# Two layers of graph attention over 64 graphs: the first two graphs in a new order, with zero products, logits from x, and TensorE transposes

## The chip, the cores and the metric

The kernel runs on one core of a Trainium2 chip, in one launch. The metric is the device time of one execution in microseconds, as the median of several runs. A separate execution was recorded by the hardware profiler; times inside the kernel are from that one.

## The reference, cut to what matters

There are 64 independent graphs of N = 256 nodes with F = 512 features, H = 8 heads of U = 64. All of it is float32.

```python
def layer0(X, A, W, b, a_self, a_neigh):                 # graph attention
    feats = einsum('bnf,hfu->bhnu', X, W)
    e_self, e_neigh = einsum('bhnu,hu->bhn', feats, a_self), einsum('bhnu,hu->bhn', feats, a_neigh)
    dense = leaky_relu(e_self[..., :, None] + e_neigh[..., None, :], 0.2)
    att = softmax(dense + -1e10 * (1.0 - A[:, None]), axis=-1)
    out = einsum('bhij,bhju->bhiu', att, feats) + b
    return relu(rows_of_heads_side_by_side(out))         # (64, 256, 512)

def layer1(x, mask, A, D, W_qkv, W_out, b_out):          # A and D are both adj here
    q, k, v = heads(x @ W_qkv)
    dots = where(mask_pair, einsum('bhid,bhjd->bhij', q, k) / 8, -big)
    attn = softmax(dots) * 0.33 + 0.33 * where(mask_pair, A, 0) + 0.33 * exp(-where(mask_pair, D, big))
    return rows_of_heads_side_by_side(einsum('bhij,bhjd->bhid', attn, v)) @ W_out + b_out

x = layernorm(x + layer0(x, adj, ...))
x = layernorm(x + layer1(x, nodemask, adj, adj, ...))
```

## The kernel before

The work on one graph is cut into named steps in six groups: `turned` (x transposed), `proj0` (features, logits and softmax factors of layer 0), `attend0` (attention of layer 0 and its normalisation), `proj1` (q, k and v of layer 1), `softmax1` and `attend1`. `do(stage, b, step)` issues one step for graph b. After each, `in_order()` ties every new instruction to the one before it on its engine, so the order in which the calls stand in `start()` and in the two loop functions is the order in which each engine executes. There is no planner. Engines wait for one another by semaphores; DMAs go to SP's queue, which takes them in order too.

The steady loop handles several graphs at once: `attention0_beside_projections1(b)` does the attention of layer 0 for graph b, q, k and v of graph b-1 and the features of graph b+1; `attention1_beside_projections0(b)` does the softmax of graph b-1 and the attention of layer 1 for graph b-2. `start()` fills this pipeline for graphs 0 and 1, then the loop runs for b = 1 to 63 and `end()` empties it.

Products of the steady loop use Strassen's scheme with seven products per two-by-two blocks (`seven`, named p1 to p7), for which VectorE prepares sums: `left_factors` of the data (steps `xC`, `hC`) and `right_factors` or `combine_weights1` of the weights. The first two graphs' features use plain products (`features(t, g)`: tile t of 128 nodes, half g of the heads), since the weight sums aren't there yet. All matmuls of L87 go through `halved`, which splits the 128 weight columns into two halves. In the records of the trace one float32 matmul is two (a transpose one).

In layer 0 the softmax needs two logits per node and head. For graph 1 and on they come as two more columns (`U:` up to `UX`) of the feature product, because `attention_vectors(g, step)` puts W times the attention vectors into the weights: step 0 transposes four weight blocks on TensorE (`pw`, L412) and copies them on ScalarE (`wT`), step 1 multiplies them with `a2` (`pwa`, L424, 4 columns), step 2 copies the result into the weights `wf` (L429). For graph 0 `logits(t, g)` computes them on VectorE from the features and `a_bc`, the attention vectors broadcast to 128 partitions (L631, L636). `copied` adds the bias and moves features out of the accumulator (L641). `maxima` transposes the logits (`pr`, L90), takes the maximum over nodes (L554) and forms the exponent; with part 1 it spreads the maxima by a product with `sel` (`pn`, L546). `columns` makes the column factors (L582, L589, L590). `factors` spreads the row factors to all partitions by products of 8 rows with `sel` (`pg`, L576); from graph 2 on, `rows` and `broadcast` do this through DRAM (`gs`, then `gb`). `scaled` scales the features on ScalarE (L649), `weights` forms the attention weights on VectorE (`pT`, L692, two per head), `product` multiplies them (`av`, L715).

Graph 0's outcome of layer 0 is divided on VectorE (L736, L738), that of the others by ScalarE: `rec0` takes reciprocals on VectorE (L728) and `norm0` scales eight heads per half on ScalarE (L746, 16 instructions). `end`, `squares` and `norm` make the layer norm. The outcome is then needed transposed for q, k and v (`hT`). For graph 0 TensorE transposes it (`from_rows`, `ph`, L90); for the others it is written to DRAM (`blocks`: `hs`, then four block loads into `hb`) and VectorE transposes it (step `hT`, L129). Values of layer 1 are `pv` (L87), copied out or added by ScalarE and VectorE (`v`, L331 and L334); the sums of the softmax are `pd` (L925). Four accumulator banks (`tag="mm"`, `bufs=4`) are shared by nearly all of these, so a product waits until a bank's last reader is done.

## Time and profile before

| | us |
|---|---|
| runs (3) | 2845.17, 2847.23, 2848.95; median 2847.23 |
| profiled execution | 2844.27, its span 2842.5 |
| TensorE busy, in the span | 2808.4 (99%) |
| VectorE, ScalarE, GpSimd busy | 2562.7, 1806.8, 252.6 |
| first feature product of graph 1 starts at | 38.69 |
| first attention product (`av`) of graph 1 | 66.63 |
| first feature product of graph 2 (`pf_p`) | 84.00 |
| first attention product of graph 2 | 111.64 |
| first value product (`pv_p`) of graph 1, of graph 2 | 122.08, 165.21 |

Times are counted from the start of the span. An execution's own time is a little longer than the span, which runs from the first to the last recorded instruction. PE is TensorE's matmuls, PEld its weight loads, DVE VectorE, ACT ScalarE, POOL GpSimd, SP the queue that issues DMAs. PEclk, or the column behind the busy times in a table of stretches, is the granted share of TensorE's full clock; behind it stand the DMA engines' busy share and GB/s. In a timeline a line gives start and length in us, engine, source line, operation, tiles, shape and count, and in brackets the idle time before it and who ended it.

### The profile page before, as it was taken

What the parts mean: (1) busy time and instruction counts of PE and PEld (TensorE: products, weight loads), DVE (VectorE), ACT (ScalarE), POOL (GpSimd) and SP (SyncE); (2) the same over time, 40 slices, a digit from 0 to 9 for tenths busy, and PEclk for the clock granted to TensorE, in tenths of its full rate; (3) what the DMA queues carried; (4) which work ended last, traced back from release to release, by engine and by line L of the source; (5) the groups of instructions that cost most, each with busy time, mean ns of one, the idle gap of its engine ahead of it and who ended that gap; (6) DMA issues with size and microseconds to landing.
All of it is one profiled execution on the core that took longest, in us unless ns stands there. A gap on an engine that the chain in (4) does not pass through costs nothing.

```text
span 2842.5 us, 93477 instructions
## 1 busy us (share of the span) xinstructions
PE 2808.4 (99%) x39110; PEld 2237.5 (79%) x39110; DVE 2562.7 (90%) x5147; ACT 1806.8 (64%) x5031; POOL 252.6 (9%) x526
## 2 busy tenths in 40 slices
PE   9899999999999999999999999999999999999998
PEld 7688787887888888877877878878778778778775
DVE  6799999999999999999999999999999999999984
ACT  3566666666666666666666666666666666666663
POOL 0001000100101000010000001001000100100011
PEclk9999999999999999999999999999999999999999
DMA  6345454454454454454554544554554545544532
GB/s 140 91 129 123 133 141 121 132 144 121 126 137 126 130 140 118 136 134 124 140 122 132 144 121 128 141 127 126 137 124 131 141 119 137 134 126 138 122 113 71
DMA packets 778972, 363.87 MB, mean 128 GB/s; under 512 B 694605, under 2 KB 696637, under 8 KB 762553
## 3 DMA queue, kind: packets, MB, share of 16 engines
q1 hardware_dynamic: 776440, 357.37, 48.3%
q8 instruction: 310, 5.08, 0.8%
q14 instruction: 110, 0.89, 0.1%
q10 hardware_dynamic: 2112, 0.52, 0.1%
HBM read 289.42 MB, written 68.13 MB: 126 GB/s over the span
## 4 chain that ended last, share of the span: by engine, by line
PE 96%; DVE 2%; DMA 1%; ACT 1%; issue 0%; SPq 0%; POOL 0%; DVEq 0%; POOLq 0%
PE pq_p L87 27%; PE po_p L87 14%; PE pf_p L87 13%; PE pv_p L87 13%; PE av L715 8%; PE pz L886 8%; PE av L1015 7%; PE pd L925 2%; PE pr L510 1%; PE po L87 0%; DMA x<-in_x_dram 0%; PE pg L576 0%; DMA hb<-hs 0%; PE pf L87 0%; SPq L122 0%
## 5 line engine op out<-in xcount | busy, mean ns | idle before, releaser
L87 PE MATMUL pq_p<-hC,wqk_sb 128*64 128x128 f32 x8192 | 472.3, 273 | 1.9 <-ACT qk L331 1.7
L87 PEld LDWEIGHTS pq_p<-hC,wqk_sb 128*64 128x64 f32 x8192 | 450.6, 137 | 4.5 <-ACT qk L331 2.8
L692 DVE SCALAR_TENSOR_TENSOR pT<-gb,ccol,at 128x256 f32<-128x256 f32 x992 | 403.0, 477 | 17.5 <-ACT ccol L589 17.5
L87 PE MATMUL pq_p<-hT,wqk_sb 128*64 128x128 f32 x6144 | 358.0, 273 | 0.0
L87 PEld LDWEIGHTS pq_p<-hT,wqk_sb 128*64 128x64 f32 x6144 | 342.4, 137 | 9.6 <-issue 0.4
L905 ACT ACTIVATE p<-pz,hide 128x512 f32<-128x512 f32 x638 | 333.6, 629 | 8.0 <-PE pz L886 1.0
L996 DVE TENSOR_TENSOR p<-p,rb 128x1024 f32<-128x1024 f32 x252 | 299.0, 1207 | 3.3 <-DMA rb<-rs 3.3
L1005 DVE TENSOR_TENSOR p<-p,ct 128x1024 f32<-128x1024 f32 x252 | 299.0, 1206 | 0.2
L746 ACT ACTIVATE x<-av,rec 128x64 f32<-128x64 f32 x1008 | 220.9, 335 | 68.3 <-DVE rec L728 68.3
L87 PE MATMUL pv_p<-wv_sb,hC 128*64 128x256 f32 x2048 | 246.7, 382 | 9.5 <-ACT v L331 9.5
L715 PE MATMUL av<-v,pT 128*64 128x65 f32 x8192 | 254.0, 223 | 1.3 <-issue 1.0
L87 PE MATMUL pf_p<-wf_sb,xC 128*64 128x264 f32 x1984 | 254.5, 386 | 0.0
L715 PEld LDWEIGHTS av<-v,pT 128*64 128x64 f32 x8192 | 250.6, 139 | 2.2 <-issue 2.0
L649 ACT ACTIVATE v<-v 128x64 f32<-128x64 f32 x1024 | 251.2, 336 | 0.0
L331 ACT COPY qk<-pq_p 128x512 f32<-128x512 f32 x256 | 149.0, 582 | 150.5 <-PE pq_p L87 147.3
L1015 PE MATMUL av<-p,v 128*64 128x256 f32 x2016 | 240.6, 379 | 2.1 <-DVE p L1005 2.1
L886 PE MATMUL pz<-qk 64*128 64x256 f32 x2048 | 238.8, 383 | 0.0
L331 ACT COPY v<-pv_p 128x256 f32<-128x256 f32 x256 | 95.7, 374 | 224.8 <-PE pv_p L87 224.8
L87 PE MATMUL po_p<-wo_sb,oC 128*64 128x256 f32 x1984 | 235.2, 379 | 0.0
L385 POOL TENSOR_SCALAR rstd_l<-rstd_l 128x2 f32<-128x2 f32 (+1 forms) x130 | 95.6, 736 | 1539.5 <-ACT junk L374 1539.5
L886 PEld LDWEIGHTS pz<-qk 64*128 64x128 f32 x2048 | 192.3, 186 | 45.1 <-issue 24.6
L87 PEld LDWEIGHTS pv_p<-wv_sb,hC 128*64 128x64 f32 x2048 | 154.9, 138 | 79.2 <-ACT v L331 10.4
(165 smaller groups left out, 4471.1 us busy)
## 6 DMA issues: line engine op xcount, KB each, us to landing
rb<-rs SPq DMA_DIRECT2D x63, 1024.0 KB
gb<-gs SPq DMA_DIRECT2D x62, 1028.0 KB
hs<-x SPq DMA_DIRECT2D x64, 512.0 KB
xb<-in_x_dram SPq DMA_DIRECT2D x252, 128.0 KB
x<-in_x_dram SPq DMA_DIRECT2D x63, 512.0 KB
hb<-hs SPq DMA_DIRECT2D x252, 128.0 KB
y<-hs SPq DMA_DIRECT2D x63, 512.0 KB
out_dram<-y SPq DMA_DIRECT2D x63, 512.0 KB
```

Of the source, the lines that this page charges most:

```text
L87: matmul(dst[cols], lhsT[:, cols], rhs, **flags)
L331: nc.scalar.copy(out[COPIES[p]], dst)
L385: nc.gpsimd.tensor_scalar(rstd, rstd, 1.0 / F, EPS, op0=ALU.mult, op1=ALU.add)
L649: nc.scalar.activation(V0[b][:, t, h, :U], V0[b][:, t, h, :U], AF.Copy, scale=V0[b][:, t, h, U : U + 1],)
L692: nc.vector.scalar_tensor_tensor(pT[h][:, j, :], GB[b][h], CCOL[b][:, j, h : h + 1], AT[b][:, j, :], op0=ALU.max, op1=ALU.mult,)
L715: matmul(av[r * half : (r + 1) * half, k, :], pT[h][:, j, i : i + half], V0[b][:, j, h, :UA], start=(j == 0), stop=(j == T - 1),)
L746: nc.scalar.activation(X1[b][:, t, h * U : (h + 1) * U], av[:, k, :U], AF.Copy, scale=REC0[g][:, t, k : k + 1],)
L886: matmul(pz[r][:, j, :], QK[b][rows, g, 1, j * P : (j + 1) * P], QK[b][rows, g, 0, :], start=True, stop=True,)
L905: nc.scalar.activation(to, of, AF.Exp, bias=hide[:, j, b : b + 1], scale=U**-0.5,)
L996: nc.vector.tensor_mul(p, p, REC[b][:, k : k + 2, g // 2, :] .unsqueeze(2) .to_broadcast([P, 2, T, N]),)
L1005: nc.vector.tensor_add(p, p, CT[b].unsqueeze(1).to_broadcast([P, 2, T, N]))
L1015: matmul(av[0][r * U : (r + 1) * U, g % 2, :], V1[b][:, j, 2 * g + r, :], PROBS[b][g][:, r, j, :], start=(j == 0), stop=(j == T - 1),)
```

## The change

Only the beginning is changed: what is done for graphs 0 and 1, and the loop, which now starts at b = 2. The instructions of the steady loop and of `end()` stay as they are.

- Zero products: `keep_busy(dst, n)` issues n matmuls of a 128x128 block of zeros with itself into an accumulator that is overwritten right after. There are 19: six before the mask's transposes, four before those of x, and for graph 0 three each before the transposes of the logits, the product that spreads the maxima and the first product that spreads the row factors. The zeros lie in `rowmask`, which is filled much later.
- Logits of graph 0 from x: all four weight blocks are transposed at once (`turned_weights`), multiplied with the attention vectors (`attention_vectors`, 16 products), copied into `wa`, and `logits()` multiplies x with that (8 products of 16 columns). `vectors_placed` copies `wa` into the weights later. The two broadcast loads of `a_bc` and VectorE's products and reductions are gone; `a2` is filled by GpSimd.
- Loads: x of graph 0 in one DMA ahead of the mask's instead of two behind it; the adjacency of graph 1 is loaded after the step `aT` at its new place.
- Order of `start()`: logits and factors come before most of graph 0's features; graph 1's row factors are spread in two halves; the weight sums for q and k come later.
- `second_beside_first()` takes the place of the loop's pass for b = 1: reciprocals and scaling of graph 1 first, VectorE's transposes of graph 2 and the sums for `wf` after or between, `right_factors` in parts.
- Graph 1's outcome is transposed by TensorE (`from_rows`), written to DRAM but not loaded as blocks.

The lines removed from `start` and `attention_vectors` are those of the listing above.

```diff
+    load_rows(0)
     mask_sb = io.tile([NB, N], U8, tag="mask", name="mask_sb", bufs=4)
     nc.sync.dma_start(mask_sb, nodemask)
-    X[0] = io.tile([P, T, F], FT, tag="hb", name="x_0", bufs=1)
-    for t in range(T):
-        nc.sync.dma_start(X[0][:, t, :], x[0, t * P : (t + 1) * P, :])
...
-    a_bc = io.tile([P, 2, H, U], FT, tag="x1", name="a_bc", bufs=1)
...
+    rowmask = consts.tile([P, NB // B, N // B, B], FT, name="rowmask")
+    idle = rowmask[:, 0, : P // B].rearrange("p i b -> p (i b)")
+    nc.vector.memset(idle, 0.0)
...
+    for r in range(2):
+        rows = slice(r * U, (r + 1) * U)
+        nc.gpsimd.tensor_copy(a2[rows, :, r, :].rearrange("p g s -> p s g"), acol[rows])
...
+    def keep_busy(dst, n):
+
+        for _ in range(n):
+            matmul(dst, idle, idle, start=True, stop=True)
+
+    keep_busy(ps_tile([P, P], "pi"), 6)
...
-    def right_factors(w, w12):
+    def right_factors(w, w12, steps=range(4)):
...
+        for i in steps:
+            if i == 0:
+                nc.vector.tensor_add(m3, w22, w12)
...
...
+    def turned_weights(g):
+
+        pw = ps_tile([P, C, P], f"pw_{g}")
+        for c in range(C):
+            for r in range(2):
+                matmul(
+                    pw[r * U : (r + 1) * U, c, :],
+                    wf[c // C2][g // 2][:, c % C2, 2 * (g % 2) + r, :U],
+                    ident,
+                    start=True,
+                    stop=True,
+                )
+        tag = "both" if g < HG - 1 else "pT"
+        wT = WA[g] = work.tile([P, C, P], FT, tag=tag, name=f"wT_{g}", bufs=4)
+        nc.scalar.copy(wT, pw)
+        in_order()
+
+    def attention_vectors():
...
+        pwa = ps_tile([P, C, HG, 4], "pwa")
+        for g in range(HG):
             for c in range(C):
+                matmul(pwa[:, c, g, :], WA[g][:, c, :], a2[:, g], start=True, stop=True)
+        wa = WA["columns"] = work.tile([P, C, H, 2], FT, tag="hC", name="wa", bufs=1)
+        nc.vector.tensor_copy(
+            wa.rearrange("p c h s -> p (c h s)"), pwa.rearrange("p c g k -> p (c g k)")
+        )
+        in_order()
+
+    def vectors_placed():
+
+        for k in range(2):
+            for g in range(2):
                 nc.vector.tensor_copy(
+                    wf[k][g][:, :, :, U:],
+                    WA["columns"][:, k * C2 : (k + 1) * C2, g * HG : (g + 1) * HG],
                 )
         in_order()
...
                 pt = ps_tile([P, C, P], f"pt_{b}_{t}")
+                if t == 0:
+                    keep_busy(pt[:, 0, :], 4)
...
         def maxima(part=None):
             if part == 1:
-                ROW["max"] = ps_tile([P, H], f"pn_{b}")
+                pn = ps_tile([P, P], f"pn_{b}")
+                if b == 0:
+                    keep_busy(pn, 3)
+                ROW["max"] = pn[:, :H]
                 matmul(ROW["max"], sel[:, H, :], ROW["diag"], start=True, stop=True)
                 return
-            ps = ps_tile([H, 2, N], f"pr_{b}")
+            ps = ps_tile([P, 2, N], f"pr_{b}")
+            if b == 0:
+                keep_busy(ps[:, 0, :P], 3)
+            ps = ps[:H]
...
-        def factors():
+        def factors(part=None):
...
+            if part != 1:
+                nc.vector.tensor_scalar(
+                    grow[:, :N], grow[:, :N], 1.0, TINY, op0=ALU.min, op1=ALU.max
+                )
+                GB[b] = []
+
+            h = HG if part == 1 else 0
+            while h < (HG if part == 0 else H):
                 n = 2 if b == 0 and h < HG else HG
                 if n == 2:
                     pg = ps_tile([P, n, N], f"pg_{b}_{h}")
                 else:
                     pg = psum.tile([P, n, N], FT, tag="sc", name=f"pg_{b}_{h}", bufs=2)
+                if b == 0 and h == 0:
+                    keep_busy(pg[:, 0, :P], 3)
                 for k in range(n):
                     matmul(pg[:, k, :], sel[:, h + k, :], grow[:, :N], start=True, stop=True)
                     GB[b].append(pg[:, k, :])
...
-        def logits(t, g):
...
+        def logits():
+
+            pl = ps_tile([P, T, H, 2], f"pl_{b}")
+            for t in range(T):
+                for c in range(C):
+                    matmul(
+                        pl[:, t],
+                        xT[:, c, t * P : (t + 1) * P],
+                        WA["columns"][:, c],
+                        start=(c == 0),
+                        stop=(c == C - 1),
+                    )
+            nc.vector.tensor_copy(V0[b][:, :, :, U:], pl)
...
         def rows_to_blocks():
             nc.sync.dma_start(HS[b].rearrange("(t p) f -> p t f", p=P), X1[b])
-            if b > 0:
+            if b > 1:
                 load_blocks(hb, HS[b])
...
         tiles = [slice(t, t + 1) for t in range(T)]
         do("proj0", 0, "xT_rows")
+        for g in range(HG):
+            turned_weights(g)
+        do("proj0", 0, "features", 0, 0)
+        attention_vectors()
+        do("proj0", 0, "logits")
+        do("proj0", 0, "copied", 0, 0)
+        do("proj0", 0, "maxima")
+        do("proj0", 0, "aT")
+        load_adj(1)
+        do("proj0", 0, "features", 1, 0)
+        do("proj0", 0, "maxima", 1)
+        do("proj0", 0, "columns")
+        do("proj0", 0, "far")
+        do("proj0", 0, "factors")
+        do("proj0", 0, "features", 0, 1)
+        do("proj0", 0, "features", 1, 1)
+        do("proj0", 0, "copied", 1, 0)
+        for h in range(HG):
+            do("proj0", 0, "scaled", h)
+            do("attend0", 0, "weights", h)
+        do("proj0", 0, "copied", 0, 1)
+        do("proj0", 0, "copied", 1, 1)
+        for h in range(HG, H):
+            do("proj0", 0, "scaled", h)
+        for t in range(T):
+            do("attend0", 0, "product", 0, t)
+        for h in range(HG, H):
+            do("attend0", 0, "weights", h)
+        vectors_placed()
+        do("turned", 1, "xT")
+        load(2)
+        for t in range(T):
+            do("attend0", 0, "product", 1, t)
         for g in range(2):
             for t in range(T):
...
+                do("proj0", 1, "features", t, g)
         for t in range(T):
             for g in range(2):
                 do("attend0", 0, "norm0", g, t)
             do("attend0", 0, "end", tiles[t])
             do("attend0", 0, "squares", tiles[t])
...
         do("proj0", 1, "copied", 0, 0)
-        combine_weights1(0)
-        do("proj0", 1, "copied", 0, 1)
-        combine_weights1(4)
         do("proj0", 1, "copied", 1, 0)
         do("proj0", 0, "shared", 0)
+        do("proj0", 1, "copied", 0, 1)
         do("proj0", 1, "aT")
         do("proj0", 1, "copied", 1, 1)
+        do("proj0", 1, "maxima")
         do("proj1", 0, "from_rows", 0)
         do("proj1", 0, "from_rows", 1)
         do("proj1", 0, "blocks")
         load_rows(1)
-        do("proj0", 1, "maxima")
-        do("proj1", 0, "qk", "p1")
         do("proj0", 1, "maxima", 1)
         do("proj0", 1, "columns")
-        do("proj1", 0, "qk", "p2")
-        do("proj1", 0, "hC")
-        do("proj0", 1, "factors")
+        do("proj1", 0, "qk", "p1")
+        do("proj0", 1, "factors", 0)
         do("proj0", 0, "shared", 1)
         do("proj0", 1, "far")
         load_adj(2)
+        combine_weights1(0)
+        combine_weights1(4)
+        do("proj1", 0, "qk", "p2")
+        do("proj1", 0, "hC")
         do("proj1", 0, "qk_add", 11)
+        do("proj1", 0, "qk", "p6")
         combine_weights1(1)
-        do("proj1", 0, "qk", "p6")
         for h in range(HG):
             do("proj0", 1, "scaled", h)
             do("attend0", 1, "weights", h)
-        combine_weights1(2)
         do("proj1", 0, "qk", "p5")
         do("proj1", 0, "qk", "p7")
+        do("proj0", 1, "factors", 1)
         for h in range(HG, H):
             do("proj0", 1, "scaled", h)
+        combine_weights1(2)
         do("proj1", 0, "qk_add", 22)
         for h in range(HG, H):
             do("attend0", 1, "weights", h)
         do("proj1", 0, "qk", "p3")
         do("proj1", 0, "qk_add", 12)
         combine_weights1(3)
...
+    def second_beside_first():
+
+
+        b = 1
+        for g in range(2):
+            for t in range(T):
+                do("attend0", b, "product", g, t)
+        do("attend0", b, "rec0", 0)
+        do("attend0", b, "rec0", 1)
+        load_rowmask()
+        nc.sync.dma_start(bo_bc, b_out.partition_broadcast(P))
+        WO["12"] = load_wo()
         do("turned", 2, "xT")
         do("turned", 2, "xC")
-        right_factors(wf_sb, wf12)
-        in_order()
+        for t in range(T):
+            do("attend0", b, "norm0", 0, t)
+        do("proj1", 0, "values", "p1")
+        for t in range(T):
+            do("attend0", b, "norm0", 1, t)
+        do("proj1", 0, "values", "p2")
+        do("proj1", 0, "v_add", 11)
+        do("attend0", b, "end")
+        right_factors(wf_sb, wf12, (0, 1, 2))
+        do("proj1", 0, "values", "p6")
+        do("proj1", 0, "values", "p5")
+        do("proj1", 0, "values", "p7")
+        do("proj1", 0, "v_add", 22)
+        right_factors(wf_sb, wf12, (3,))
+        load(3)
+        do("proj0", 2, "product", "p1")
+        do("proj1", 0, "values", "p4")
+        do("attend0", b, "squares", slice(0, 1), False)
+        do("proj0", 2, "product", "p6")
+        do("attend0", b, "squares", slice(1, 2), slice(0, 2))
+        do("proj1", 0, "values", "p3")
+        do("proj0", b, "shared")
+        do("proj0", 2, "aT")
+        do("proj1", 0, "v_add", 12)
+        do("proj0", 2, "product", "p5")
+        do("proj0", 2, "product", "p7")
+        do("attend0", b, "norm")
+        do("proj1", b, "blocks")
+        do("proj0", 2, "add", 22)
+        do("proj0", 2, "product", "p2")
+        do("proj0", 2, "product", "p4")
+        do("proj0", 2, "far")
+        do("proj0", 2, "product", "p3")
+        do("proj0", 2, "add", 11)
+        right_factors(wo_sb, WO["12"], (0, 1))
+        do("proj0", 2, "add", 12)
+        do("proj1", b, "from_rows", 0)
+        do("proj1", b, "from_rows", 1)
+        do("proj0", 2, "shared", 0)
+        do("proj0", 2, "rows")
+        right_factors(wo_sb, WO.pop("12"), (2, 3))
+        do("proj0", 2, "broadcast", 0)
+        do("softmax1", 0, "scores", 0)
+        do("proj0", 2, "broadcast", 1)
+        load_adj(3)
+        do("softmax1", 0, "scores", 1)
+        do("proj0", 2, "shared", 1)
+        do("proj1", b, "hC")
+        do("softmax1", 0, "both", 0)
+        do("softmax1", 0, "scores", 2)
+        do("softmax1", 0, "both", 1)
+        do("softmax1", 0, "scores", 3)
+        do("softmax1", 0, "both", 2)
+        do("turned", 3, "xT")
+        do("softmax1", 0, "both", 3)
+        do("proj1", b, "qk", "p1")
+        do("proj1", b, "qk", "p2")
+        do("proj0", 2, "bias")
+        do("softmax1", 0, "sums")
+        do("softmax1", 0, "invert")
+        do("proj0", 2, "columns")
+        do("softmax1", 0, "inverted")
...
     start()
-    for b in range(1, NB):
+    second_beside_first()
+    for b in range(2, NB):
         attention0_beside_projections1(b)
         attention1_beside_projections0(b)
     end()
```

## The prediction

> **What bounds the kernel now.** I read the page first, for the engine shares and the row of the granted clock; then TensorE's waits over the first 125 us; then a table of busy time over stretches cut where the clock steps; then the timeline of the places that stood out.

> ```profile
> span 2842.5 us, 93477 instructions
> PE 2808.4 (99%) x39110; PEld 2237.5 (79%) x39110; DVE 2562.7 (90%) x5147; ACT 1806.8 (64%) x5031; POOL 252.6 (9%) x526
> ```

> TensorE is busy for 99%, so over the long loop only TensorE work counts, and the change takes none of it away. What it can win lies where TensorE idles or runs slowly. The waits of the first 125 us (engine and line, waited for, us in total, times, longest):

> ```profile
> PE pv_p L87 <- ACT v L331: 7.0, 1, 7.0
> PE pm L90 <- DVE maskf L211: 3.8, 1, 3.8
> PE pd L925 <- DVE both L917: 3.0, 3, 2.0
> PE pt L90 <- DMA x<-in_x_dram: 1.5, 1, 1.5
> ```

> About half of the kernel's 34 us without TensorE lies here. The table by stretches (busy us and counts by engine, then the granted clock):

> ```profile
> 22.10:32.34 10.24, 10.24 (x82) 8.34 (x80) 7.20 (x19) 3.54 (x15) 0.00 (x0) 0.50 1.10 216
> 35.75:39.17 3.42, 3.42 (x46) 3.09 (x43) 2.94 (x9) 1.40 (x3) 0.72 (x2) 1.00 0.60 97
> 52.82:56.23 3.41, 3.41 (x30) 2.80 (x30) 3.41 (x7) 1.54 (x3) 0.00 (x0) 1.00 0.17 40
> 56.23:59.65 3.42, 3.42 (x38) 3.42 (x36) 2.86 (x6) 1.52 (x6) 0.00 (x0) 0.50 0.43 145
> 66.63:76.71 10.08, 5.63 (x148) 4.74 (x144) 9.91 (x20) 1.15 (x6) 0.00 (x0) 1.00 0.56 128
> 76.71:84.00 7.29, 4.73 (x24) 2.67 (x26) 3.00 (x8) 2.88 (x13) 0.23 (x1) 0.53 0.04 6
> 84.00:111.64 27.64, 24.02 (x290) 17.65 (x288) 19.75 (x41) 15.51 (x40) 1.10 (x3) 1.00 0.48 115
> 111.64:122.08 10.44, 9.34 (x198) 8.34 (x196) 10.22 (x22) 5.89 (x26) 0.00 (x0) 1.00 0.58 133
> 122.08:165.21 43.13, 43.13 (x611) 33.94 (x608) 37.45 (x76) 25.44 (x75) 1.32 (x4) 1.00 0.38 107
> ```

> From 122 us on TensorE never stops: 43.1 us a graph. Before that it works at half clock three times (10.2, 3.4 and 6.8 us, that is 10.2 us lost), and idles 4.4 us up to 76.71, 2.6 to 84, 3.6 to 111.6. The clock's records begin at 11.86; before, TensorE runs at half clock too: the weight loads of the first features come in pairs 0.43 us apart until 11.7, and later four pairs take 0.86. Why the 7.0:

> ```profile
> 69.99 1.23 DVE L129 STREAM_TRANSPOSE xT<-xb 128x1024 f32<-128x1024 f32 x1
> 72.73 0.70 DVE L226 TENSOR_TENSOR wf_sb<-wf_sb,wf 128x528 f32<-128x528 f32 x1
> 75.33 0.27 DVE L728 RECIPROCAL rec<-av 128x8 f32<-128x8 f32 x2
> 75.56 3.39 ACT L746 ACTIVATE x<-av,rec 128x64 f32<-128x64 f32 x16 [9.87 <-DVE rec L728]
> 79.27 4.90 PE L87 MATMUL pv_p<-wv_sb,hC 128*64 128x256 f32 x24 [7.01 <-ACT v L331]
> ```

> The reciprocal of graph 1 stands behind 5 us of transposes and weight sums on VectorE, its 16 scalings hold ScalarE, and behind these waits the copy that frees the bank of the next value product.

> **The change part by part**, stage by stage to the landmark from which both kernels run the same loop (first value product of graph 1, 122.08 us before).

> *Stage 1, to the first feature product of graph 1 (before: 38.69).* A 128x128 zero product has no row. Below it stands the attention-vector product (same weights, 4 columns moved; 16 records in 1.95 us, 0.24 each of 8), above it the broadcast product (256 columns; 3.72 for 8, 0.465 each). By columns moved I take 0.35, and 0.7 at half clock. The six first ones (4.2 us) run before x can be there: cost nothing, covered by its transfer; without that cover 4.2. x comes in one 512 KB transfer issued at 0.7 instead of two up to 2.4; the two landed for 5.8 and 6.8, I take 6.2. The mask now queues behind it, so its transposes come at about 7.0 instead of 3.8 and end at 7.3; TensorE stands behind them in order. The clock's steps lie 3.41 us apart, so 5.03 and 8.45 precede 11.86; with the zero products filling 1.6 to 5.0, I take full clock from 8.45 (before: 11.86). Of four zero products 1.6 run at half clock till then, the rest take 0.8 (9.3); the eight transposes of x, 1.0 (10.3). Then 32 transpositions of weights, 3.8 (row: 16 in 1.91), 14.1; a feature product 1.72, 15.8, hiding the four ScalarE copies of 0.59; 16 attention-vector products 3.8, 19.6; the VectorE copy and its hand-overs 0.4; eight logit products at 0.25, 2.0, 22.0; three zero products 1.05, of which about 0.5 covers the copy to V0; transposes of logits 0.44, 23.5; features 1.72, hiding reduction, exponent and diagonal (0.41+0.14+0.21); three zeros and the maxima product, 26.5; three zeros, hiding columns (0.18 and 0.22 on ScalarE), 27.6; broadcasts 3.72, 31.3; features 3.44, 34.7; attention product 1.87, 36.6. VectorE can copy the last features only at 34.9 (0.42) and then make eight weight rows at 0.41, to 38.6; the second attention product 1.87 waits for them, 40.5. The four placing copies (0.15 each) and graph 1's transpose (1.23) on VectorE end just with it. So **+1.8**: VectorE's logits (8 instructions, 5.4 us) are gone, but ran beside TensorE; their replacement is a chain on TensorE. The two copies into a2 go from VectorE (0.34) to POOL, idle then: nothing. The adjacency load of graph 1 now waits on SP for a later transpose of graph 0's, and the x blocks of graph 2 behind it; both are used 15 us later.

> *Stage 2, to graph 1's attention product (before 27.94).* The same products, 24.8 us: features 7.1, seven products of 1.75, broadcasts 3.72, transposes 1.5, maxima 0.24. Before, half clock cost 1.7 and waits 1.4. The broadcasts now come in two halves of 1.86 among full-width products, so I drop the half clock; waits of about 1.1 stay (hand-overs of row maxima and hT). 25.9: **-2.0**.

> *Stage 3, to graph 2's first product (before 17.37).* Attention 3.73 and five value products of 0.864, 4.3. The reciprocals stand ahead of graph 2's transposes; eight scalings (8x0.25) now stand between two ScalarE copies instead of sixteen behind a late reciprocal, so two waits of 0.7 come in place of the 7.0. 9.4: **-7.9**, of which 2.4 is clock lost after the idling. The 5 us of VectorE work is late next, under 3 us of value products; the last right factor only must precede graph 2's p2 and p4, far off.

> *Stage 4, to graph 2's attention product (before 27.64).* The four block loads, the 1.25 VectorE transpose and the trip through DRAM give way to eight TensorE transposes (1.02) and two ScalarE copies (0.54 each). Products: 8.0, transposes 1.5, scores 3.65, sums 1.0, qk 8.75, and 1.0 of waits for the last pair sums, now behind two qk products: 23.9, **-3.7**. On SP the write of graph 2's row factors no longer queues behind four block loads.

> *Stage 5 (before 10.44).* Bound by VectorE's weights, 16 x 0.41 and an addition, in both: **0**.

> Sum: 1.8 - 2.0 - 7.9 - 3.7 = **-11.8**. The profiled execution, 2844.27 (span 2842.5 and 1.8 around it), becomes 2832.5; the median of the runs is 3.0 above it, so 2847.23 becomes **2835.4**.

> [...] The row of 52.82:56.23 does not: TensorE was busy for all of it and the clock was halved after it. 2.5 us of it were broadcasts that use 8 of 128 rows; 0.9 was full-width. So some busy work counts for little. [...] If work with nothing in it counts as nothing, they hold nothing: first rival. A row speaks for the forecast: 35.75:39.17 kept its clock with only 0.7 us of attention and feature products in it, less than the 0.9; the rest were transpositions of weights (moving an identity, nearly all zeros) and 4-column vector products (1.88). One of the two must count, and the zero products resemble both.

> **The rivals.**
> *Half clock in stage 1.* Vector products, logits, zeros and broadcasts run from 15.8 to 31.3 with one feature product in between. If they count like the broadcasts, full clock comes at 11.86 as before (+1.8) and three steps at half clock cost 5.1: **2842.3**; two steps without the delay, 3.4. For: the row of 52.82. Against: that of 35.75.
> *Late factors.* Before, 11.4 us passed from issuing gs (97.37) to the first use of gb; now about 9.5 are left between the clipped row and the weights. Up to 1.9 lost: **2837.3**. VectorE was busy elsewhere before, so the true trip is shorter.
> *Slower.* Neither zeros nor transposes count: full clock comes only at 18.69, when the transpositions of weights have filled a step (they end at 19.2 instead of 14.1, +5.1), and the 15.5 us from vector products to broadcasts double. 2835.4 + 20.6 = **2856.0**. It decides from a loss of 11.8, that is 23.6 us more at half clock. Against: the feature products inside alone should lift it.
> *The zeros do nothing*, clock as without them: then the thirteen not hidden are mere cost, in the sum already at about 4 to 6.

> **How the numbers follow.** The forecast 0.58, half clock 0.25, late factors 0.10, slower 0.05, others 0.02. 0.2% is 5.7 us, about what a measurement of this kernel can tell from no change: 2841.5 is the edge, so over half of the second case is "same". Faster 0.81, same 0.14, slower 0.05. Low end: clock full a step earlier (-0.6), zero products at 0.24 (-1.4), smaller waits in stages 2 to 4 (-2.9): 2830.5. High end: half clock with some late factors, 2843.

> **What would show it.** Right: no half clock after the first 9 to 12 us; first feature product of graph 1 at 40 to 42; no wait over 1 us before pv_p; graph 1's transposes on TensorE before pz; the landmark at 109 to 112 instead of 122.08. Wrong: half clock between 16 and 34; a wait for gb before graph 2's attention; a period other than 43.1.

## The result, and the profile after

| us | before | after |
|---|---|---|
| median of the runs of one comparison | 2845.84 (2843.49 to 2848.95, 8 runs) | 2838.76 (2836.10 to 2841.22, 8 runs) |
| profiled execution, its span | 2844.27, 2842.5 | 2838.85, 2837.1 |
| first feature product of graph 1 | 38.69 | 47.33 |
| first value product of graph 1 | 121.91 | 116.09 |

The ratio of the times is 0.9976, with a 95% interval of 0.9965 to 0.9987: faster by 7.1 us, where 11.8 were forecast. The page after, its first lines:

```profile
span 2837.1 us, 93579 instructions
PE 2813.9 (99%) x39172; PEld 2231.9 (79%) x39172; DVE 2556.9 (90%) x5135; ACT 1805.0 (64%) x5033; POOL 252.6 (9%) x528
```

TensorE is still busy for 99% of the span, and its busy time even rose from 2808.4 to 2813.9 us. What became shorter is its idle time. TensorE's waits over the first 125 us (engine and line, waited for, us in total, times, longest):

```profile
PE pm L90 <- DVE maskf L215: 2.6, 1, 2.6
PE av L747 <- DVE pT L724: 1.9, 1, 1.9
PE pq_p L87 <- ACT hT L880: 0.4, 1, 0.4
PE pd L957 <- DVE both L949: 0.3, 1, 0.3
```

The 7.0 us of pv_p are gone, and 3.0 of pd shrank to 0.3. The 1.9 ahead of graph 0's second attention product is the one that the forecast had put at 2.0. The table of busy time by stretches, cut at the steps of the clock and at the landmarks of the forecast (start and end; length; busy us and counts of PE, PEld, DVE, ACT, POOL; granted clock; DMA share; GB/s):

```profile
12.67:16.09 3.42, 3.42 (x58) 3.12 (x56) 0.00 (x0) 2.30 (x4) 0.00 (x0) 1.00 0.80 126
16.09:19.50 3.41, 3.41 (x33) 2.87 (x29) 0.00 (x0) 0.00 (x0) 0.00 (x0) 1.00 0.54 79
19.50:29.74 10.24, 9.92 (x47) 8.40 (x48) 2.06 (x7) 0.46 (x1) 0.00 (x0) 0.50 1.35 225
29.74:33.16 3.42, 3.42 (x26) 2.59 (x23) 0.70 (x3) 1.02 (x4) 0.00 (x0) 1.00 1.37 217
33.16:36.57 3.41, 3.41 (x17) 2.63 (x18) 2.65 (x7) 2.65 (x10) 0.00 (x0) 1.00 0.69 89
36.57:39.98 3.41, 3.41 (x18) 1.96 (x16) 0.71 (x3) 0.00 (x0) 0.00 (x0) 0.50 0.00 0
47.33:73.79 26.46, 25.67 (x326) 21.88 (x323) 22.47 (x51) 12.40 (x34) 3.28 (x8) 1.00 0.44 102
73.79:82.27 8.48, 8.46 (x173) 6.43 (x171) 7.77 (x18) 3.92 (x18) 0.00 (x0) 1.00 0.48 121
82.27:106.50 24.23, 23.89 (x298) 18.65 (x296) 23.02 (x50) 16.64 (x43) 1.88 (x4) 1.00 0.37 93
106.50:116.09 9.59, 9.17 (x196) 8.19 (x194) 9.55 (x22) 4.71 (x21) 0.00 (x0) 1.00 0.91 220
116.09:159.20 43.11, 42.65 (x598) 34.48 (x596) 37.24 (x76) 25.13 (x73) 1.32 (x4) 1.00 0.38 107
```

The last five rows are stages 2 to 5 and one graph of the loop. Stages 2 to 4 became shorter much as forecast, and the period is the same (43.11 after 43.13). The six rows above them lie in stage 1. Two of them are at half clock, 13.65 us together; the clock's records begin at 12.675. A step is 3.413 us, the grid of the clock's records in this profile (6.827, 10.241, 6.827 and 3.412 us). In the step 16.09:19.50 TensorE is busy for the whole of its 3.41 us, and the next three steps are at half clock. What it was busy with, from the timeline of TensorE (start us, us, engine, line, operation, out and in, count of records, idle before and releaser):

```profile
15.14 1.89 PE L87 MATMUL pf<-wf_sb,xT 128*64 128x256 f32 x16
16.97 4.71 PE L437 MATMUL pwa<-a,wT 128*128 128x4 f32 x32
22.00 3.60 PE L663 MATMUL pl<-wa,xT 128*128 128x16 f32 x16 [0.32 <-DVE wa L439]
25.43 1.63 PE L211 MATMUL pr<-rowmask 128*128 128x128 f32 x6
30.64 0.94 PE L211 MATMUL pn<-rowmask 128*128 128x128 f32 x6
32.68 3.72 PE L606 MATMUL pg<-grow,sel 8*128 8x256 f32 x16
45.44 2.09 PE L747 MATMUL av<-v,pT 128*64 128x65 f32 x64 [1.89 <-DVE pT L724]
```

The products of 4 columns (pwa, 16.97 to 19.50) and of 16 columns (pl, from 22.00), and the broadcasts that use 8 rows (pg, 32.68 to 36.4), stand ahead of or in the half clock. A zero product leaves two records: three take 0.94 at full clock (the rows overlap a little; about 0.29 each) and 1.63 at half (0.54, with what follows overlapping; six on end at the start took 2.93, 0.49 each).

The part that had carried the wait of 7.0 us, as it stands now on VectorE and ScalarE:

```profile
77.14 0.20 DVE L760 RECIPROCAL rec<-av 128x8 f32<-128x8 f32 x1
77.38 1.75 ACT L778 ACTIVATE x<-av,rec 128x64 f32<-128x64 f32 x8 [4.53 <-DVE rec L760]
77.91 1.25 DVE L129 STREAM_TRANSPOSE xT<-xb 128x1024 f32<-128x1024 f32 x1
82.22 0.70 DVE L232 TENSOR_TENSOR wf_sb<-wf_sb,wf 128x528 f32<-128x528 f32 x1
```

The reciprocals now come ahead of graph 2's transpose and of the weight sums, eight scalings at a time.

### The profile page after: what moved, and what is told of

The parts are those of the page before. It is cut to its first block, busy times and chain, and to the rows that moved or that the text cites. A ratio compares the mean times of both kernels' runs of the same rounds, so it can differ in the third digit from the quotient of the medians.

```text
span 2837.1 us, 93579 instructions
## 1 busy us (share of the span) xinstructions
PE 2813.9 (99%) x39172; PEld 2231.9 (79%) x39172; DVE 2556.9 (90%) x5135; ACT 1805.0 (64%) x5033; POOL 252.6 (9%) x528
## 4 chain that ended last, share of the span: by engine, by line
PE 97%; DVE 1%; DMA 1%; ACT 1%; issue 0%; POOL 0%; SPq 0%; DVEq 0%; POOLq 0%; ACTq 0%
PE pq_p L87 27%; PE po_p L87 14%; PE pf_p L87 13%; PE pv_p L87 13%; PE av L747 8%; PE pz L918 8%; PE av L1047 7%; PE pd L957 2%; PE pr L531 1%; PE pf L87 1%; PE po L87 0%; DMA x<-in_x_dram 0%; PE pg L606 0%; DMA mask_sb<-in_nodemask_dram 0%; PE pwa L437 0%
## 5 line engine op out<-in xcount | busy, mean ns | idle before, releaser
L87 PE MATMUL pq_p<-hC,wqk_sb 128*64 128x128 f32 x8192 | 469.7, 273 | 1.1 <-ACT qk L340 1.1
L87 PEld LDWEIGHTS pq_p<-hC,wqk_sb 128*64 128x64 f32 x8192 | 448.6, 137 | 2.3 <-ACT qk L340 1.5
L87 PE MATMUL pq_p<-hT,wqk_sb 128*64 128x128 f32 x6144 | 357.7, 273 | 0.4 <-ACT hT L880 0.4
L87 PEld LDWEIGHTS pq_p<-hT,wqk_sb 128*64 128x64 f32 x6144 | 342.0, 137 | 10.1 <-issue 0.7
L87 PE MATMUL pf_p<-wf_sb,xC 128*64 128x264 f32 x1984 | 253.6, 386 | 0.1
L87 PE MATMUL pv_p<-wv_sb,hC 128*64 128x256 f32 x2048 | 244.1, 379 | 2.5 <-ACT v L340 2.5
L87 PE MATMUL po_p<-wo_sb,oC 128*64 128x256 f32 x1984 | 235.2, 379 | 0.0
L949 DVE SCALAR_TENSOR_TENSOR both<-p 128x512 f32<-128x512 f32 x256 | 172.4, 675 | 46.5 <-ACT p L937 46.2
```

The lines of the kernel that those rows point to most:

```text
L87: matmul(dst[cols], lhsT[:, cols], rhs, **flags)
L949: nc.vector.scalar_tensor_tensor(both[g], p[:, :, 0, :], TINY, p[:, :, 1, :], op0=ALU.add, op1=ALU.add)
```

## The experiments

The time of each is the median of its runs. The kernel before ran in the same comparisons: 2846.39 (27 runs) with the first four kernels, 2846.29 (33 runs) with the next four, 2846.19 (9 runs) with the last. The start of graph 1's first feature product in the profiled execution is the finer measure of stage 1. It has a scatter of its own: three executions with the same start (the changed kernel and the two that alter only its second stage, through DRAM and with the reciprocals late) have it at 47.33, 47.20 and 46.61. The time behind the first value product of graph 1, the same work in all, varies more. In some executions the last 80 us have one to three steps of half clock before the kernel runs out of work: in the seven profiles with such steps that rest takes 2721.8 to 2726.1 us, in the four without 2720.6 to 2721.0. The same wait of 2.50 us stands there in all eleven profiles. In the changed kernel no half clock followed it; in the kernel without zero products it did, and the products behind it took 1.98 us instead of 1.08:

```profile
2802.57 1.08 PE L87 MATMUL pv_p<-wv_sb,hC 128*64 128x256 f32 x8 [2.50 <-ACT v L340]
2803.24 1.98 PE L87 MATMUL pv_p<-wv_sb,hC 128*64 128x256 f32 x8 [2.50 <-ACT v L337]
```

**No zero products.** All the calls of keep_busy fall away; the order is the changed kernel's.

```diff
-    keep_busy(ps_tile([P, P], "pi"), 6)
 def keep_busy(dst, n):
-        for _ in range(n):
-            matmul(dst, idle, idle, start=True, stop=True)
+        return
```

> The changed kernel without its 19 zero products. Theory A (zero products count as work, the products that move 4 to 16 columns do not): about 4 us of TensorE work leave the path (four at half clock 1.9, nine at full clock 0.29 each less the 0.5 that covers the copy), but the step of the clock's grid that holds the products for maxima and row factors loses its filling, so the clock is half right after it and 2 to 4 us come back: 2837 to 2840, and the granted clock is half for more of the time before 45 us than the 13.7 us of the changed kernel behind the start. Theory B (zero products count for nothing): the clock steps stay as in the changed kernel, and the time falls by the 4 us: about 2835.

2841.73 us (2837.62 to 2844.98), ratio 0.9983 [0.9976, 0.9989]; first feature product of graph 1 at 45.60.

```profile
17.75:27.99 10.24, 9.64 (x46) 7.72 (x47) 2.06 (x7) 0.46 (x1) 0.00 (x0) 0.50 1.21 207
27.99:31.41 3.42, 2.96 (x18) 2.20 (x15) 1.52 (x6) 2.30 (x8) 0.00 (x0) 1.00 1.37 218
31.41:38.23 6.82, 6.82 (x26) 4.09 (x26) 2.48 (x8) 1.37 (x6) 0.00 (x0) 0.50 0.60 86
```

Without the zeros the first loss is the same (10.24 us at half clock), and the second is two steps (6.82) instead of one. So the zeros at pn and pg saved one step, worth 1.7 us, but all the zeros together cost more than that: stage 1 is 1.7 us shorter without any. Part of these 1.7 can be the place of the grid, since full clock began at 10.93 here and between 11.7 and 12.7 in the three executions with zeros. More half clock without the zeros was theory A's sign; neither theory's time came. The median is 3 us longer than the changed kernel's, not shorter. The profiled execution has another 6.8 us at half clock from 2803 on, among the last products of the kernel, which both kernels share and which in the changed kernel's profile stayed at full clock. That is 3.4 us in this execution; whether it is also what parts the medians (20 runs against 8), and why it should come more often without zeros, stays open.

**Wide zero products at the start.** Five of 512 columns instead of six of 128.

```diff
-    keep_busy(ps_tile([P, P], "pi"), 6)
+    pi = ps_tile([P, F], "pi")
+    for _ in range(5):
+        matmul(pi, idle, wide, start=True, stop=True)
```

> The first six zero products (128 columns moved) become five that move 512 columns each, so that TensorE moves columns for nearly all of the time until x lands. Theory A: full clock comes one or two steps earlier, at 6 to 9.5 us instead of 12.7, and the first 8 us of products after the mask run faster: 1.5 to 2 us less, about 2837. Theory B: full clock comes at the same step (12 to 13 us), and the time is that of the changed kernel, 2838.8, or up to 1 us more, because the five end after the mask has landed.

2837.50 us (2835.66 to 2838.86), ratio 0.9971 [0.9961, 0.9982]; first feature product of graph 1 at 45.72.

```profile
1.44 6.41 PE L216 MATMUL pi<-rowmask 128*128 128x512 f32 x10 [1.44 <-DVE a L175]
```

```profile
1.78:5.20 3.42, 3.42 (x5) 1.36 (x5) 0.93 (x7) 1.28 (x1) 0.00 (x0) 1.00 1.00 244
5.20:15.43 10.23, 10.23 (x106) 7.46 (x104) 1.12 (x4) 3.41 (x6) 0.39 (x2) 1.00 0.99 155
15.43:18.85 3.42, 3.42 (x33) 3.42 (x32) 0.00 (x0) 0.00 (x0) 0.00 (x0) 1.00 0.59 98
18.85:29.09 10.24, 9.92 (x46) 7.27 (x45) 2.06 (x7) 0.47 (x1) 0.00 (x0) 0.50 1.32 226
```

The clock's first record is a full one at 5.195 (the 1.00 of the first row has no record under it; the records of 512 columns start 0.85 us apart up to there and 0.43 apart from 5.5 on), and up to there TensorE had run nothing but zero products. So in this run products of zeros by zeros were enough for full clock at 5.195. The other half of the dispute is in the third row, 3.42 us of vector products of 4 columns and nothing else, with no idle time and weight loads busy for all of it (PEld 3.42): three steps at half clock follow. Full clock 7.5 us earlier brought only 1.6 us: the five long products hold TensorE until 7.85, so the mask's transposes start at 7.78 instead of 6.53, and the loss in the middle stayed.

**Features between the vector products.** The same work in another order: half of the vector products, a feature product, the other half, and so on; the broadcasts in two groups with features between.

```diff
         do("proj0", 0, "features", 0, 0)
-        attention_vectors()
...
+        attention_vectors(0)
+        do("proj0", 0, "features", 1, 0)
...
+        attention_vectors(1)
+        do("proj0", 0, "features", 0, 1)
...
         do("proj0", 0, "logits")
...
-        do("proj0", 0, "factors")
-        do("proj0", 0, "features", 0, 1)
-        do("proj0", 0, "features", 1, 1)
+        do("proj0", 0, "factors", 0)
+        do("proj0", 0, "features", 1, 1)
+        do("proj0", 0, "factors", 1)
```

> The same products of graph 0 in another order: feature products stand between the two halves of the attention-vector products, ahead of the logits, and between the two halves of the row factors. Nothing is added or left out. Theory A (the half clock of 19.5 to 29.7 and 36.6 to 40 comes of steps filled with products that move few columns or use 8 rows): no step lies long enough in such products, half clock nearly disappears behind 13 us, and 4 to 6 us are won: 2833 to 2835. Rival (the new chain's length, not the clock, makes stage 1 long): the order of equal work changes the end by less than 1.5 us: 2837.5 to 2839.

2832.82 us (2832.13 to 2834.48), ratio 0.9958 [0.9943, 0.9973]; first feature product of graph 1 at 40.71.

```profile
9.53:26.60 17.07, 17.07 (x180) 14.16 (x178) 2.25 (x8) 3.43 (x6) 0.38 (x2) 1.00 1.04 175
26.60:30.01 3.41, 3.26 (x19) 2.56 (x20) 1.81 (x7) 3.03 (x10) 0.00 (x0) 1.00 1.34 220
30.01:33.43 3.42, 3.42 (x17) 1.57 (x17) 2.43 (x7) 1.34 (x6) 0.00 (x0) 0.50 0.86 155
33.43:40.71 7.28, 5.88 (x138) 5.26 (x138) 5.60 (x16) 1.78 (x7) 0.00 (x0) 1.00 0.18 31
```

One step at half clock is left, after 26.60:30.01 with its broadcasts. The start lies 6.6 us earlier with the same instructions, and the rival's time (2837.5 or more) did not come. 40.71 is close to what the forecast had said (40.5) for a stage 1 at full clock, though it still holds the 1.7 us of that step.

**The old start with the new second stage.** What graph 0 did at the start of before, and the transposes on TensorE and the order of second_beside_first from the change.

```diff
     start()
-    for b in range(1, NB):
+    second_beside_first()
+    for b in range(2, NB):
```

> The start of the kernel before (no zero products, logits on VectorE, old order, old loads), with the changed kernel's own stage for graph 1 and TensorE's transposes. Theory A: the gain behind graph 1's attention product (42.3 us in the changed kernel against 55.5) does not depend on the start: 2845.8 - 13 = 2833, below the changed kernel. Rival: the new start pays for it (its order leaves VectorE with less to do later, and graph 1's weights earlier): part of the 13 is lost, 2836 to 2840.

2834.30 us (2831.28 to 2835.51), ratio 0.9960 [0.9946, 0.9975]; first feature product of graph 1 at 39.00.

```profile
22.18:32.42 10.24, 10.24 (x81) 8.24 (x79) 7.55 (x19) 3.76 (x16) 0.00 (x0) 0.50 1.13 214
56.31:59.73 3.42, 3.42 (x38) 3.42 (x36) 3.09 (x7) 1.08 (x4) 0.00 (x0) 0.50 0.64 156
66.94:75.42 8.48, 8.46 (x173) 6.43 (x171) 7.99 (x19) 3.92 (x18) 0.00 (x0) 1.00 0.46 121
75.42:99.66 24.24, 23.90 (x299) 18.66 (x297) 23.04 (x50) 16.64 (x43) 1.88 (x4) 1.00 0.37 93
```

Stages 3 and 4 take 8.48 and 24.24 us, as in the changed kernel (8.48 and 24.23), and the half clock of before at 22 and 56 is back. So the gain of these stages is the second stage's own and does not rest on the new start; what is new up to graph 1's attention product cost 4.5 us by the medians (8 runs against 4 here), 5.0 by the profiled spans. The time lies between the two expectations, nearer to theory A.

**Graph 1 through DRAM.** The changed kernel, with its outcome turned as before.

```diff
-        if b > 1:
+        if b > 0:
             hb = io.tile([P, C, N // B, B], FT, tag="hb", name=f"hb_{b}", bufs=1)
...
-        do("proj1", b, "from_rows", 0)
-        do("proj1", b, "from_rows", 1)
...
+        do("proj1", b, "hT")
         do("proj1", b, "hC")
```

> The changed kernel, with graph 1's outcome turned as before: through DRAM and by VectorE's transposes (ahead of hC) in place of TensorE's. Theory (the step of stage 4 in the prediction: the way through DRAM is what cost there): stage 4, from graph 2's first feature product (82.27 in the changed kernel) to its attention product, goes from 24.2 back to 26 to 28 us, with a wait of 2 to 4 us ahead of graph 1's pq_p, the rest stays; 2841 to 2843. Rival (the transposes' cost moved from VectorE to TensorE one for one, and the gain of stage 4 is the order alone): stage 4 at 23 to 24.5, since the eight transposes (1.1 us) and their idle time are gone from TensorE, 2838 to 2839.

2843.55 us (2840.25 to 2849.20), ratio 0.9993 [0.9986, 0.9999].

```profile
PE pq_p L87 <- DVE hT L129: 4.9, 1, 4.9
```

```profile
98.03:104.86 6.83, 4.55 (x44) 4.55 (x46) 5.78 (x10) 0.59 (x1) 0.00 (x0) 0.50 0.76 195
82.15:112.45 30.30, 24.75 (x291) 19.81 (x289) 24.80 (x52) 16.19 (x42) 1.87 (x4) 0.89 0.42 92
```

The wait came, longer than expected, and it brought two steps at half clock that none of the expectations had. Stage 4 is 30.3 instead of 24.23 us, above the 26 to 28 expected and 2.7 above the kernel before (27.64): 4.9 for the wait, less 1.1 for the eight transposes, and some 2.3 for what ran at half clock after 100.3.

**The reciprocals late.** The changed kernel, with rec0 of graph 1 behind graph 2's transposes and the four sums of wf_sb.

```diff
-        do("attend0", b, "rec0", 0)
-        do("attend0", b, "rec0", 1)
...
         do("turned", 2, "xT")
         do("turned", 2, "xC")
+        right_factors(wf_sb, wf12)
+        do("attend0", b, "rec0", 0)
+        do("attend0", b, "rec0", 1)
```

> The changed kernel, with the reciprocals of graph 1's attention (rec0) put behind graph 2's transposes xT, xC and the four sums of wf_sb on VectorE, as they stood behind such work before. Theory (stage 3 of the prediction: what stood ahead of the reciprocals on VectorE was the wait for v of 7.01 us ahead of pv_p): the wait ahead of pv_p comes back with 5 to 7 us, stage 3 goes from 8.5 to 13.5 to 15.5, and the time is 2844 to 2846. Rival (the wait went because pv_p got other PSUM tiles to write or because ScalarE was free earlier): stage 3 stays within 1 us, 2838 to 2840.

2844.25 us (2842.54 to 2847.31), ratio 0.9991 [0.9982, 0.9999].

```profile
PE pv_p L87 <- ACT v L340: 5.4, 1, 5.4
```

```profile
73.07:88.05 14.98, 9.61 (x174) 7.13 (x171) 10.44 (x21) 4.04 (x18) 0.23 (x1) 0.89 0.42 89
```

Stage 3 takes 14.98 us, within the theory's 13.5 to 15.5, and one of its steps is at half clock. Where the two reciprocals stand on VectorE is worth 6.5 us of TensorE's time here.

**No gap at the start.** The kernel with features between the vector products, with three wide zero products up to x's landing, the mask turned behind x, and two zero products ahead of the weights' transposes.

```diff
-    keep_busy(ps_tile([P, P], "pi"), 6)
+    pi = ps_tile([P, F], "pi")
+    for _ in range(3):
+        matmul(pi, idle, wide, start=True, stop=True)
...
         do("proj0", 0, "xT_rows")
+        mask_columns()
...
-                if t == 0:
-                    keep_busy(pt[:, 0, :], 4)
...
+        if g == 0:
+            keep_busy(pw[:, 0, :], 2)
```

> The kernel with features between the vector products (2832.8), in which the start is closed up as well: three zero products of 512 columns (3.9 us) up to x's landing at 5.0, x turned at once, the mask turned behind it, and two zero products ahead of the weights' transposes in place of four ahead of x's. Theory A (zero products count, products of few columns or rows don't): full clock from 5 to 9 us, the weights' transposes start at 8.4 to 9 (when their last block lands) instead of 9.93, graph 1's first feature product at 38.5 to 39.7 instead of 40.71, time 2830.5 to 2832. Theory B (zero products count for nothing): no full clock before 10, first feature product at 40 or later, time 2832 to 2835.

2830.87 us (2830.20 to 2832.81), ratio 0.9944 [0.9931, 0.9956]; first feature product of graph 1 at 37.35.

```profile
5.98:37.35 31.37, 29.83 (x360) 24.30 (x360) 12.87 (x39) 9.57 (x28) 0.39 (x2) 1.00 0.99 164
```

Full clock from 5.978 on, through the whole of stage 1. The time is what theory A said; the start is 1.2 us earlier than its range, because the last step at half clock of the kernel it was built on went too. Its median is the lowest of the study.

**The old start with zero products.** They go among graph 0's row transposes and broadcasts; graph 1's broadcasts are parted in two.

```diff
+                    keep_busy(pn, 3)
...
+                keep_busy(ps[:, 0, :P], 4)
...
+                if b == 0 and h > 0:
+                    keep_busy(pg[:, 0, :P], 3 if h < HG else 4)
...
-        do("proj0", 1, "factors")
+        do("proj0", 1, "factors", 0)
...
+        do("proj0", 1, "factors", 1)
```

> The kernel with the start of before and the second stage of the change (2834.3, first feature product of graph 1 at 39.00, half clock 22.2 to 32.4 and 56.3 to 59.7): 14 zero products (4.1 us at full clock) go among its row transposes and broadcasts (4 ahead of pr, 3 ahead of pn, 3 and 4 between the pg of graph 0), and the broadcasts of graph 1 are parted in two groups of four. Theory A: the clock stays full or halves for one step of 3.4 us in place of three, which gives back 3.4 to 5.1 us for the 4.1 spent, of which 0.9 lie in waits; first feature product at 36.5 to 39; the half clock at 56 goes (-1.7); time 2830 to 2832.5. Theory B (zero products count for nothing): half clock at 22 as before, and 14 zero products at 0.3 to 0.6 us each more; first feature product at 42 to 45, time 2836 to 2839.

2835.91 us (2834.12 to 2838.46), ratio 0.9962 [0.9948, 0.9975]; first feature product of graph 1 at 44.14.

```profile
12.62:26.27 13.65, 13.19 (x121) 10.10 (x118) 10.97 (x26) 6.46 (x21) 0.00 (x0) 1.00 0.90 163
22.86:26.27 3.41, 3.10 (x15) 2.20 (x16) 3.08 (x8) 3.28 (x15) 0.00 (x0) 1.00 0.99 212
26.27:39.93 13.66, 13.66 (x122) 12.08 (x124) 5.76 (x18) 1.57 (x6) 0.00 (x0) 0.50 0.83 161
```

Neither expectation came true as it stood. The half clock at 22 did not come, which speaks against theory B; but it came at 26.27 and stayed for four steps, and the start is within the range of B, the time at its edge. Only the second part did its work: the half clock at 56 is gone. That full clock had come behind zero products alone (5.195, in the wide start) was not enough to place them by. I then counted, in the timelines of the ten kernels so far up to 75 us, what each step from the first record of the clock on holds of full-width products (those that move 64 columns or more through all 128 rows: features, transpositions of x and of weights, attention, qk and value products, zeros, and the row transposes, though these fill only 8 columns of weights), taking broadcasts, vector, logit, maximum and mask products as nothing. In these ten profiles the record of the clock in the next step goes with that count:

| step runs at | full-width products in it | next step | steps |
|---|---|---|---|
| full clock | 1.2 us or less | half | 16 |
| full clock | 1.46 us or more | full | all others |
| half clock | up to 2.7 us | half | 18 |
| half clock | 2.7 us and above | full | all others |

No step of those counted is an exception at full clock. Here 22.86:26.27 held about 1.0 us, and the four steps at half clock held about 1.8, 1.3, 2.4 and 2.7. In the changed kernel, 16.09:19.50 held 0.88 and 33.16:36.57 held 0.24, while 29.74:33.16 held 2.6 thanks to its six zero products. Records of 512 columns start 0.85 us apart at half clock and 0.43 at full (the wide start), so both borders speak of about the same amount of columns: by these times 2.7 us at half clock are about 1.37 at full. A step of the changed kernel with 1.52 us of attention products and 1.89 of waiting, at 43.4, kept the clock.

Outside these steps the profiles differ from the table in two things. At half clock the border is not sharp. In this kernel the step 5.79:9.21, ahead of the first record, held 2.95 us and half clock still followed (the weight loads of the features come in pairs 0.43 us apart up to 11), and near the end of three kernels 2.73, 2.81 and 2.87 were not enough either. And "all 128 rows" is too narrow. Up to 75 us there are no score products; in the loop there are (pz, 64 rows, 256 columns), and some steps hold nothing else. In the changed kernel:

```profile
176.32 3.73 PE L918 MATMUL pz<-qk 64*128 64x256 f32 x32
176.52:179.93 3.41, 3.41 (x32) 2.81 (x30) 3.41 (x8) 3.28 (x7) 0.00 (x0) 1.00 0.95 150
```

The clock stayed full behind this step, as it did behind all 38 such steps of the eleven kernels. So these products of 64 rows have to be counted, whether in whole or in half these steps do not tell; behind 33.16:36.57, with about 3.2 us of broadcasts of 8 rows, half clock followed. With 64 rows counted in whole, the steps at full clock part in the same way over the whole length of all eleven profiles: each of the 9004 steps followed by full clock held 1.46 us or more, and of the 39 followed by half clock 38 held 1.38 or less. The one exception held 1.54 (the kernel with graph 1 through DRAM, at 2763.84). These borders were read off the steps that they describe and say nothing of other kernels; the next kernel was planned with them, on the count up to 75 us.

**Zero products placed by that count.** 2 for 4 ahead of pr, and three more ahead of the first pg.

```diff
-                keep_busy(ps[:, 0, :P], 4)
+                keep_busy(ps[:, 0, :P], 2)
...
-                if b == 0 and h > 0:
+                if b == 0:
                     keep_busy(pg[:, 0, :P], 3 if h < HG else 4)
```

> The kernel with the old start and zero products, its zeros placed by the count that the runs so far give: at full clock a step of 3.41 us with 1.46 us or more of products that use all 128 rows and 64 columns or more kept the clock, one with 1.19 us or less lost it. Here 2 (for 4) ahead of pr, 3 ahead of pn, and 3, 3 and 4 among the pg, the first 3 of these partly in a wait of 0.47 us; every stretch of 3.4 us then holds at least 1.7 us. Theory A with this count: no half clock between 12 and 75 us; first feature product at 37 to 38.5 (39.00 with the old start, less 5.1 for the half clock, plus 15 times 0.29, less what lies in waits); 2830 to 2832. Rival (what a step needs is not such products but few waits, or the broadcasts throttle whatever lies beside them): half clock from 22 to 27 on for two steps or more, first feature product at 42 or later, 2835 or more.

2832.13 us (2830.73 to 2838.16), ratio 0.9956 [0.9942, 0.9970]; first feature product of graph 1 at 37.21.

```profile
9.52:37.21 27.69, 26.73 (x335) 21.78 (x331) 19.62 (x52) 9.22 (x28) 0.25 (x2) 1.00 0.95 165
```

One zero product more than in the kernel above (15 for 14), otherwise placed, and the start is 6.9 us earlier, with full clock throughout. This is the count's own test, forecast before the run, and the clock did what it said. The least that a step held was about 1.5 us, not the 1.7 expected, and so near the border. The median is 0.1 above the range; one of the five runs took 2838.16 at a mean clock of 0.996, where the others had 0.998, so some of it ran at half clock; where, no profile shows. The run also tells what the new start is worth. The old start needs 37.21 us with full clock from 9.5, and the new one, at its best here, 37.35 with full clock from 6.0. Both have zero products, so this is not a clean comparison, but logits and vectors on TensorE show no gain over logits on VectorE.

## Why the prediction was right, and where not

The sign, the size within its range and the place of the gain came out; the sum was 4.7 us too good on the difference of the medians and 6.4 on the profile (2832.5 forecast, 2838.85 measured). That the total fell into the range is in part luck. The case that the forecast was made for, a stage 1 without half clock, did not happen: what came was the rival that had been given 0.25, and its 6.8 us were softened by 1.9 in stages 3 and 5 that nobody had forecast. Of the signs of being right, no wait over 1 us ahead of pv_p and graph 1's transposes on TensorE came; no half clock after 12 us, 40 to 42 for graph 1's first feature product and 109 to 112 for the landmark (116.09) did not. Of the signs of being wrong, half clock between 16 and 34 came. By its steps:

- *Stage 1, forecast +1.8: wrong, +8.6.* The step that failed is the clock, at full from 8.45 on. The rival "half clock in stage 1" came true: full clock began at 12.675, and half clock returned at 19.50 and at 36.57 for 10.24 and 3.41 us. Against the forecast that is 2.1 for the late begin, 5.1 and 1.7: 8.9 us. Against it stands 2.1 that the forecast had put too high: the zero products at 0.29 instead of 0.35 make 0.5 of it over nine, x's transposes at 8.77 instead of 9.3 another 0.5; what the rest is stays open. The failing assumption within the step: I asked whether transpositions and vector products count together, found from the row 35.75:39.17 that one of them must, and let both count. By the count above it was the transpositions of weights (with the attention and feature products 1.53 us in that step); a step of 3.42 us of vector products alone (15.43:18.85 in the wide start) was followed by half clock, and they and the logits run for two steps on end.
- *Zero products hold the clock: an estimate of the forecast, and right* in the wide start, where full clock came at 5.195 behind zero products alone. They failed where they were few: none stood among the vector products and the logits (16.97 to 25.4), where the loss of 10.24 us began.
- *Six zeros at the start cost nothing: right in cost, wrong in use.* They were put at 0.7 each and at 1.6 to 5.0; they took 0.49, ended at 4.0, and a gap of 2.6 us followed, because the mask landed behind x; the step 2.44 to 5.85 held 1.5 us of them at half clock, less than the 2.7 of the count.
- *Stage 2, forecast -2.0: -1.5.* The half clock at 56 went, as said, but the products took 25.67 us where 24.8 were put. That it was the broadcasts parted in two is supported by the old start with zeros, where the parting came with that loss gone as well.
- *Stage 3, forecast -7.9: -8.9.* The two waits of 0.7 us did not come: TensorE idled 0.02 us, and its products took 8.46 where 8.0 were put. That the reciprocals' place was the cause is shown by the late reciprocals.
- *Stage 4, forecast -3.7: -3.4.* The way through DRAM shows that the order alone does not bring it: without TensorE's transposes it leaves a wait of 4.9 and a longer stage than before.
- *Stage 5, forecast 0: -0.85*, of which 0.17 is only where I had cut before (its row begins at 121.91, not 122.08). The rest was not followed up.
- The rival "late factors" fell: no wait for gb, stage 4 within 0.4 of the forecast. "Slower" fell at once: full clock came at 12.675 and not at 18.69, behind a step (9.26:12.67) that held the transpositions of x and of the weights alone; in the wide start it came behind zeros alone. "The zeros do nothing" fell too, though in the changed kernel they earned one step of clock (1.7 us) and, by one profile of each, cost about 1.7 more than it.

Idle time alone does not part the steps. In the changed kernel three steps in a row were at half clock after a step with no idle time at all (16.09:19.50, with 0.88 us of full-width products), and the clock stayed after a step with 1.89 us of waiting (43.4, with 1.52). Behind the wait of 2.50 us near the end half clock followed in seven of eleven profiles.

## What to carry to other kernels

Ask of each stretch of TensorE not only whether it is busy: read its granted clock beside the shapes of its products, as here, where steps with 1.46 us or more of products of 64 columns and 64 rows or more were followed by full clock. A vector product of 4 columns took 0.12 us a record at full clock, and a broadcast of 8 rows and 256 columns 0.23, about as long as the two halves of a feature product of 256 (0.22), and steps filled with the one (15.43:18.85 in the wide start) or the other (33.16:36.57 in the changed kernel) were followed by half clock. So reductions that moved from VectorE to TensorE as narrow products had a price in clock here: 10.24 us at half clock, 5.1 us lost, behind the first of them. What helped was to put wide products that are due anyway between them (6.6 us, for an order alone), and zeros in the steps that still fell short (6.9 us by their places). When a short instruction frees a long chain on another engine, as the reciprocals did, its place in the queue is worth more than its length: 6.5 us for two instructions of 0.2.
